# Statistics of two norms in a window-attention and Fourier kernel: one matmul with constant weights, an extra column of queries and keys, and row sums placed ahead of the keys

## The chip, the cores and the metric

The kernel runs on one core of a Trainium2 chip. Its time is device microseconds from the first to the last instruction of an execution; the median of several executions is compared. The engines of the core have names that come back in every profile line: PE (TensorE, matrix products; PEld is its loading of weights), DVE (VectorE), ACT (ScalarE), POOL (GpSimd) and SP (which here only issues DMAs). Each engine works through its own instructions in order and waits for others through semaphores.

## The reference, cut to what matters

The input x has 32 images of 56 x 56 positions with 128 channels, in 32-bit floats. Two layers are applied, each as x = x + layer(group norm of x):

```
def _gn(v, G=32, eps=1e-5):        # 32 groups of 4 channels
    m, s = mean and variance over height, width and the 4 channels of a group
    return (v - m) / sqrt(s + eps)

x = x + window_attention(_gn(x))   # 7x7 windows, shifted by 3, 4 heads of 32
x = x + fourier_layer(_gn(x))      # 32 cosine modes along w and along h, then a feed-forward 128-512-128
```

In the attention q, k and v are linear in the normed input, without a bias of their own: q = Wq (x - m) r = (Wq r) x - (Wq r) m, where r is the reciprocal deviation of a channel's group. So the norm can be put into the weights (scaled by r) and a shift (the product of weights and -m r). The statistics of the second norm are sums and sums of squares over an image's result of the first layer.

## The kernel before, in words

An image is held as 28 chunks of 112 positions x 128 channels (`xl`, positions on partitions). `image_group` (L252) transposes one row of eight windows at a time into `xw` (channels on partitions, 392 positions, and 15 columns of zeros behind them) and takes statistics of each (`bn_stats`, L270).

The main loop (L857) runs in cycles, one for each row of windows: eight cycles per image, 256 in all, and a tail. A cycle overlaps several stages of a software pipeline. Row r gets queries, keys, values and scores in cycle r, is normalised by its softmax in cycle r+1, and is transposed, multiplied with the values, projected and added to `xl` in cycle r+2. In cycle r+3 its sums for the second norm are taken (`attn_sums`, instructions at L501 and L503). Beside that the Fourier layer of the image before (from cycle 10 on: `CONV_BEGIN`) and the feed-forward of the image before that are spread over the same cycles. The feed-forward (`ff_in`, L688; `ff_out`, L708) takes part in cycles with numbers 7 to 10 and 12 to 14 of an image's Fourier schedule, which runs over 16 cycles, so in the steady state in seven cycles of eight.

The order on PE, ACT, DVE and POOL is written out by hand: the instructions run in the order in which the functions emit them (L850). `full_first` (L764) opens a cycle: transposes of the attention weights (`attn_transpose`, L411 to L421), queries and keys (`attn_qk`), a step of the first norm of the next image, the row sums (`attn_sums`), the statistics of the second norm where the image's Fourier layer begins (`fourier_stats`), the first half of the feed-forward, and the softmax's division (`attn_divide`, L397 to L400). Then come the scores (L367) with their eviction on DVE (L375), the values (L345), the Fourier transforms and mixes, and last the second half of the feed-forward and the projection (L478) with its eviction into `xl` (L486).

PSUM is used through two rings of four banks each: `pa` for the attention and both norms, `pc` for the Fourier layer and the feed-forward.

The places that the change touches:

- `image_norm` (L278): a chain of small steps, spread over two cycles before an image's first row. Group means by a matmul with `gavg` (L284), deviations, group variance by another (L295), `rstd` by POOL (L299), `nb` = -mean x rstd (L301), weights `wn` = `wqkv` x rstd on ACT (L306), then three matmuls of one column each for the shifts of q, k and v (L309), and DVE writes the five columns of `bqkv` from them (L313 to L315): shift of q times its scale, of k, of v, and of k masked for even and odd heads.
- `attn_qk` (L319): a 392-column matmul for q (L323) and for k (L328). ACT evicts q (L324) and half of k (L330) with their shifts as bias; DVE evicts the other half of k (L333).
- `attn_sums`: ACT squares the piece (L501), then DVE reduces the piece and the squares, both by line L503, into `part`.
- `fourier_stats`: DVE adds the eight rows (`tot`, L513) and copies each group's sums to its four channels (`totc`, L521). Two matmuls with `totc` as weights and a single column `gmean` give mean and mean square per channel (L525). DVE copies them (`ms`, L533) and goes on to the variance (L535, L539), POOL gives `rstd` (L543), DVE the shift (L545).

Of the kernel before, what the change touches and what calls it, by code (L numbers as in the profile page):

```python
# [10 lines left out]
F32 = mybir.dt.float32  # L11
AF = mybir.ActivationFunctionType
ALU = mybir.AluOpType
AX = mybir.AxisListType

P = 128
S = 56
C = 128
# [12 lines left out]
TC = 2 * S  # L31
# [17 lines left out]
def swin_fourier_kernel(  # L49
# [166 lines left out]

    gmean = const.tile([TC, 1], F32, tag="gmean", name="gmean")
    nc.gpsimd.memset(gmean, 1.0 / (4 * NT))
# [59 lines left out]
    def image_norm(im):  # L278
# [6 lines left out]
        gm = small.tile([P, 1], F32, tag="gm", name="gm")  # L285
        nc.vector.tensor_copy(gm, pg[:, 0:1])
        d = small.tile([P, 1], F32, tag="d", name="d")
        nc.vector.tensor_tensor(d, mv[:, 0:1], gm, ALU.subtract)
# [18 lines left out]
        pb = attn_bank()  # L307
        for j in range(3):
            nc.tensor.matmul(  # L309
                pb[:, j : j + 1], lhsT=wqkv[:, j * C : (j + 1) * C], rhs=nb, start=True, stop=True  # L310
            )
        im.bias = small.tile([P, 5], F32, tag="bqkv", name="bqkv")
        nc.vector.tensor_scalar(im.bias[:, 0:1], pb[:, 0:1], QS, None, ALU.mult)  # L313
        nc.vector.tensor_copy(im.bias[:, 1:3], pb[:, 1:3])
        nc.vector.tensor_scalar(im.bias[:, 3:5], heads, im.bias[:, 1:2], None, ALU.mult)  # L315
        yield


    def attn_qk(im, i):  # L319

        q, src = q_sb, im.xw[i][:, :RT]
        pq = attn_bank()
        nc.tensor.matmul(pq[:, :RT], lhsT=im.w[:, 0:C], rhs=src, start=True, stop=True)  # L323
        nc.scalar.activation(  # L324
            q[:, :RT], pq[:, :RT], AF.Identity, bias=im.bias[:, 0:1], scale=QS
        )
        pk = attn_bank()
        nc.tensor.matmul(pk[:, :RT], lhsT=im.w[:, C : 2 * C], rhs=src, start=True, stop=True)  # L328
        pk3 = pk[:, :RT].rearrange("p (w j) -> p w j", j=WT)
# [166 lines left out]
    def attn_sums(im, i):  # L496

        n0, n1 = WS * i // 2, WS * (i + 1) // 2
        piece = im.x[:, n0:n1]
        sq = work.tile([TC, 4, C], F32, tag="sq", name="sq", bufs=1)  # L500
        nc.scalar.activation(sq[:, : n1 - n0], piece, AF.Square)  # L501
        for k, src in ((0, piece), (1, sq[:, : n1 - n0])):
            nc.vector.tensor_reduce(  # L503
                im.part[:, k, :, i],
                src.rearrange("p n (g c) -> p g n c", c=4),
                axis=AX.XY,
                op=ALU.add,
            )


    def fourier_stats(im):
# [6 lines left out]
        )  # L518

        totc = small.tile([TC, 2, C // 4, 4], F32, tag="totc", name="totc", bufs=1)  # L520
        nc.vector.tensor_copy(totc, tot.unsqueeze(3).to_broadcast([TC, 2, C // 4, 4]))  # L521
        yield
        pg = attn_bank()
        for k in range(2):
            nc.tensor.matmul(  # L525
                pg[:, k : k + 1],
                lhsT=totc[:, k].rearrange("p g c -> p (g c)"),
                rhs=gmean,
                start=True,
                stop=True,  # L530
            )
        ms = small.tile([P, 2], F32, tag="ms", name="ms")
        nc.vector.tensor_copy(ms, pg[:, 0:2])  # L533
        nm2 = small.tile([P, 1], F32, tag="nm2", name="nm2")
# [215 lines left out]
    def row(r):  # L750
        return (images[r // NWR], r % NWR) if 0 <= r < NB * NWR else (None, 0)
# [12 lines left out]
    def full_first(cycle, norm):  # L764
        im, i = row(cycle - 2)
        if im:
            attn_transpose(im, i, cycle - 2)
        im, i = row(cycle)
        if im:
# [4 lines left out]
        next(norm)  # L774
        im, i = row(cycle - 3)
        if im:
            attn_sums(im, i)
        for im, c in fourier(cycle):
# [160 lines left out]
```

## Time and profile before

| what | value |
|---|---|
| time, median of 3 runs | 3755.23 us (3753.02 to 3755.56) |
| span of the profiled execution | 3748.9 us |
| mean granted PE clock | 0.993 |
| q and k matmuls (L323, L328) | 512 passes each, mean 509 and 506 ns |
| bias matmuls (L309) | 192 passes, mean 244 ns |
| statistics matmuls of the second norm (L525) | 128 passes, mean 251 ns; PE idle before them 17.2 us |
| row sums (L503), 384 and 512 wide | 545 ns and 678 ns, 128 each of piece and squares |
| keys on DVE (L333) | 256 of 685 ns; DVE idle before them 420.0 us |

A matmul of 32-bit floats shows as two passes, each with a weight load (PEld) that overlaps the passes around it. In a line of the profile `out<-in` gives the tiles by the program's names, then shapes, then how many instructions stand behind the line; what follows the bar is busy time, the mean of one, and the engine's idle time just before it with what ended it. In a timeline the columns are start and length in us, engine, line, operation, and in brackets the idle time before. DMA queues are busy 36.7% of the span.

### The profile page before, as it was taken

What the parts mean: (1) busy time and instruction counts of PE and PEld (TensorE: products, weight loads), DVE (VectorE), ACT (ScalarE), POOL (GpSimd) and SP (SyncE); (2) the same over time, 40 slices, a digit from 0 to 9 for tenths busy, and PEclk for the clock granted to TensorE, in tenths of its full rate; (3) what the DMA queues carried; (4) which work ended last, traced back from release to release, by engine and by line L of the source; (5) the groups of instructions that cost most, each with busy time, mean ns of one, the idle gap of its engine ahead of it and who ended that gap; (6) DMA issues with size and microseconds to landing.
All of it is one profiled execution on the core that took longest, in us unless ns stands there. A gap on an engine that the chain in (4) does not pass through costs nothing.

```text
span 3748.9 us, 140497 instructions
## 1 busy us (share of the span) xinstructions
PE 3658.2 (98%) x61632; PEld 2985.1 (80%) x61632; DVE 2197.3 (59%) x4619; ACT 2131.1 (57%) x3809; POOL 1370.9 (37%) x1421
## 2 busy tenths in 40 slices
PE   6799999999999999999999999999999999999998
PEld 5678888888888788888878888888887888888776
DVE  6665665556655556655556655666556566655641
ACT  3455556555565556555555565555655555655553
POOL 4333343333434333343334333333343333333321
PEclk8899999999999999999999999999999999999999
DMA  4233334334333434343343343343333333433332
GB/s 111 78 100 106 107 91 116 105 103 114 91 111 105 110 99 112 96 110 106 104 111 100 98 115 104 100 114 94 110 105 107 103 112 92 115 106 104 94 104 89
DMA packets 687779, 388.95 MB, mean 104 GB/s; under 512 B 40479, under 2 KB 658112, under 8 KB 686912
## 3 DMA queue, kind: packets, MB, share of 16 engines
q1 hardware_dynamic: 686557, 379.65, 36.7%
q8 instruction: 485, 7.95, 0.9%
q14 instruction: 126, 1.03, 0.1%
q10 hardware_dynamic: 611, 0.32, 0.0%
HBM read 218.29 MB, written 161.48 MB: 101 GB/s over the span
## 4 chain that ended last, share of the span: by engine, by line
PE 88%; DVE 7%; ACT 2%; DMA 1%; issue 1%; POOL 0%; SPq 0%; ACTq 0%; POOLq 0%; DVEq 0%
PE pc L708 20%; PE pc L688 15%; PE pa L345 7%; PE pc L572 6%; PE pc L606 5%; PE pa L367 5%; PE pa L411 5%; PE pa L478 5%; PE pc L645 5%; PE pa L436 4%; PE pa L323 4%; PE pa L328 4%; PE pa L259 2%; DVE part L503 1%; DVE st L270 1%; DVE a L375 1%
## 5 line engine op out<-in xcount | busy, mean ns | idle before, releaser
L400 POOL TENSOR_TENSOR a<-a,rs 128x784 f32<-128x784 f32 x256 | 389.5, 1521 | 1366.7 <-DVE rs L399 1254.4
L708 PE MATMUL pc<-wff,hid 128*128 128x128 f32 (+1 forms) x6400 | 778.2, 279 | 0.9 <-ACT hid L696 0.7
L708 PEld LDWEIGHTS pc<-wff,hid 128*128 128x128 f32 (+1 forms) x6400 | 731.0, 189 | 21.0 <-issue 1.9
L688 PE MATMUL pc<-xf,wff 128*128 128x512 f32 (+2 forms) x1792 | 712.8, 540 | 0.0
L696 ACT ACTIVATE hid<-pc,b1sb 128x512 f32<-128x512 f32 (+2 forms) x896 | 540.9, 634 | 102.0 <-PE pc L688 98.7
L688 PEld LDWEIGHTS pc<-xf,wff 128*128 128x128 f32 x1792 | 337.1, 190 | 300.4 <-issue 229.5
L386 POOL TENSOR_TENSOR a<-a,mx 128x784 f32<-128x784 f32 x256 | 389.0, 1520 | 389.2 <-DVE mx L385 384.7
L717 DVE TENSOR_TENSOR res<-pc,res 128x512 f32<-128x512 f32 (+2 forms) x256 | 143.5, 571 | 597.1 <-issue 269.8
L333 DVE TENSOR_SCALAR k<-pa,heads,bqkv 128x392 f32<-128x392 f32 x256 | 175.4, 685 | 420.0 <-ACT k L330 419.9
L419 ACT COPY aT<-pa 113x452 f32<-113x452 f32 x256 | 137.3, 536 | 475.4 <-PE pa L411 475.3
L274 POOL TENSOR_TENSOR xl<-xl,bproj 112x384 f32<-112x384 f32 (+1 forms) x256 | 291.4, 1139 | 227.3 <-PE pa L259 224.2
L392 ACT ACTIVATE a<-a 128x784 f32<-128x784 f32 x256 | 222.6, 869 | 203.5 <-POOL a L386 202.3
L375 DVE TENSOR_TENSOR a<-pa,bm 128x392 f32<-128x392 f32 x512 | 259.5, 549 | 132.1 <-PE pa L367 132.1
L352 ACT COPY v<-pa 128x512 f32<-128x512 f32 x256 | 152.4, 595 | 295.6 <-PE pa L345 295.6
L467 DVE TENSOR_SCALAR oT<-pa,bqkv 128x98 f32<-128x98 f32 (+2 forms) x768 | 171.1, 279 | 248.0 <-PE pa L436 248.0
L678 POOL TENSOR_TENSOR res<-res,b2sb 128x512 f32<-128x512 f32 (+2 forms) x256 | 263.8, 1036 | 101.0 <-DMA res<-scr 101.0
L367 PEld LDWEIGHTS pa<-k,q 64*64 64x64 f32 x8192 | 184.0, 133 | 142.7 <-issue 52.9
L345 PE MATMUL pa<-wn,xw 128*64 128x128 f32 x4096 | 282.1, 280 | 1.1 <-ACT aT L419 1.1
L345 PEld LDWEIGHTS pa<-wn,xw 128*64 128x64 f32 x4096 | 220.0, 137 | 55.3 <-issue 21.9
L478 PE MATMUL pa<-wproj,oT 128*112 128x128 f32 x1792 | 239.3, 274 | 14.3 <-DVE oT L467 11.3
L411 PE MATMUL pa<-ident,a 113*113 113x113 f32 x2048 | 250.0, 265 | 1.5 <-POOL a L400 1.5
L367 PE MATMUL pa<-k,q 64*64 64x98 f32 x8192 | 233.4, 250 | 18.5 <-DVE k L333 18.5
(87 smaller groups left out, 5939.7 us busy)
## 6 DMA issues: line engine op xcount, KB each, us to landing
zscr<-z SPq DMA_DIRECT2D x512, 112.0 KB
htok<-scr SPq DMA_DIRECT2D x256, 196.0 KB
zT<-zscr SPq DMA_DIRECT2D x192, 256.0 KB
res<-scr SPq DMA_DIRECT2D x160, 256.0 KB
out_dram<-res SPq DMA_DIRECT2D x128, 256.0 KB
scr<-xl SPq DMA_DIRECT2D x128, 224.0 KB
xl<-in_x_dram SPq DMA_DIRECT2D x32, 784.0 KB
xl<-in_x_dram SPq DMA_DIRECT2D x32, 672.0 KB
```

What stands on the lines that cost most here:

```text
L274: nc.gpsimd.tensor_tensor(piece, piece, bproj.unsqueeze(1).to_broadcast([TC, n1 - n0, C]), ALU.add)
L345: nc.tensor.matmul(pv[hs, j * C : (j + 1) * C], lhsT=im.xw[i][:, w * WT : w * WT + JP], rhs=im.w[:, 2 * C : 3 * C], start=True, stop=True,)
L367: nc.tensor.matmul(ps[hp][HALVES[e], pr * 2 * WT : (pr + 1) * 2 * WT], lhsT=q[cs, w * WT : w * WT + JP], rhs=k_sb[cs, :, w], start=True, s ...
L375: nc.vector.tensor_tensor(a[:, 2 * hp : 2 * hp + 2, :, 0:WT].rearrange("p u w j -> p w u j"), ps[hp][:, :RT].rearrange("p (w u j) -> p w u ...
L386: nc.gpsimd.tensor_tensor(a3, a3, mx.unsqueeze(2).to_broadcast([P, 2 * NWR, WT]), ALU.subtract)
L400: nc.gpsimd.tensor_tensor(a3, a3, rs.unsqueeze(2).to_broadcast([P, 2 * NWR, WT]), ALU.mult)
L411: nc.tensor.transpose(pt[:PW, h * P : h * P + PW], a[:PW, h, 2 * hf : 2 * hf + 2].rearrange("p w j -> p (w j)")[:, :PW], ident[:PW, :PW],)
L478: nc.tensor.matmul(pp[:TC, (n - n0) * C : (n - n0 + 1) * C], lhsT=oT[:, (n - base) * TC : (n - base + 1) * TC], rhs=wproj, start=True, sto ...
L678: nc.gpsimd.tensor_tensor(res[:m, c0:c1], res[:m, c0:c1], b2sb[:m].unsqueeze(1).to_broadcast([m, c1 - c0, C]), ALU.add,)
L688: nc.tensor.matmul(ph[:, :n], lhsT=wff1[:, f * P : (f + 1) * P], rhs=xff[:, t0 : t0 + n], start=True, stop=True,)
L696: nc.scalar.activation(hf[:, :n], ph[:, :n], AF.Relu, bias=b1sb[:, f : f + 1])
L708: nc.tensor.matmul(pf[:m, c * C : (c + 1) * C], lhsT=im.hid[f][:, c * P : c * P + m], rhs=wff2[:, f], start=(f == 0), stop=(f == NF - 1),)
```

## The change

There are three edits.

1. The second norm's statistics. `gmean` becomes a 112 x 128 block of one constant and is the weights; `tot` itself (64 columns: 32 sums, 32 sums of squares) is streamed, by one matmul in place of two. Every channel then holds all 64 group values; DVE multiplies them by a mask of the channel's own group (from `gavg`, with its 0.25 undone by a factor 4) and reduces to the two values. The copy `totc` goes.
2. The first norm's shifts of q and k. Minus the group mean is written as column 392 of the first row's `xw`, so that the q and k matmuls of that row, made 393 columns wide, give the shifts as their last column. ACT takes these from PSUM into `bqkv`: one small operation ahead of q, two ahead of k, in the first row of each image alone. Only the shift of v keeps its own matmul.
3. The row sums. `attn_sums` becomes a generator in two parts. The reduce of the piece itself is emitted between `attn_transpose` and `attn_qk`, so that on DVE it stands between `aT` and the keys; the squares on ACT and their reduce stay where they were.

The order of the instructions on PE, POOL and SP is the same but for the matmuls that are left out.

```diff
@@ -214,7 +214,7 @@
     mhalf = const.tile([P, 1], F32, tag="mhalf", name="mhalf")
     nc.gpsimd.memset(mhalf, -0.5)
 
-    gmean = const.tile([TC, 1], F32, tag="gmean", name="gmean")
+    gmean = const.tile([TC, P], F32, tag="gmean", name="gmean")
     nc.gpsimd.memset(gmean, 1.0 / (4 * NT))
 
 
@@ -284,6 +284,8 @@
         nc.tensor.matmul(pg[:, 0:1], lhsT=gavg, rhs=mv[:, 0:1], start=True, stop=True)
         gm = small.tile([P, 1], F32, tag="gm", name="gm")
         nc.vector.tensor_copy(gm, pg[:, 0:1])
+
+        nc.vector.tensor_scalar(im.xw[0][:, RT : RT + 1], gm, -1.0, None, ALU.mult)
         d = small.tile([P, 1], F32, tag="d", name="d")
         nc.vector.tensor_tensor(d, mv[:, 0:1], gm, ALU.subtract)
         e = small.tile([P, 1], F32, tag="e", name="e")
@@ -305,27 +307,28 @@
         yield
         nc.scalar.mul(im.w, wqkv, rstd)
         pb = attn_bank()
-        for j in range(3):
-            nc.tensor.matmul(
-                pb[:, j : j + 1], lhsT=wqkv[:, j * C : (j + 1) * C], rhs=nb, start=True, stop=True
-            )
+        nc.tensor.matmul(pb[:, 0:1], lhsT=wqkv[:, 2 * C :], rhs=nb, start=True, stop=True)
         im.bias = small.tile([P, 5], F32, tag="bqkv", name="bqkv")
-        nc.vector.tensor_scalar(im.bias[:, 0:1], pb[:, 0:1], QS, None, ALU.mult)
-        nc.vector.tensor_copy(im.bias[:, 1:3], pb[:, 1:3])
-        nc.vector.tensor_scalar(im.bias[:, 3:5], heads, im.bias[:, 1:2], None, ALU.mult)
+        nc.vector.tensor_copy(im.bias[:, 2:3], pb[:, 0:1])
         yield
 
 
     def attn_qk(im, i):
 
-        q, src = q_sb, im.xw[i][:, :RT]
+        n = RT if i else RT + 1
+        q, src = q_sb, im.xw[i][:, :n]
         pq = attn_bank()
-        nc.tensor.matmul(pq[:, :RT], lhsT=im.w[:, 0:C], rhs=src, start=True, stop=True)
+        nc.tensor.matmul(pq[:, :n], lhsT=im.w[:, 0:C], rhs=src, start=True, stop=True)
+        if i == 0:
+            nc.scalar.mul(im.bias[:, 0:1], pq[:, RT:n], QS)
         nc.scalar.activation(
             q[:, :RT], pq[:, :RT], AF.Identity, bias=im.bias[:, 0:1], scale=QS
         )
         pk = attn_bank()
-        nc.tensor.matmul(pk[:, :RT], lhsT=im.w[:, C : 2 * C], rhs=src, start=True, stop=True)
+        nc.tensor.matmul(pk[:, :n], lhsT=im.w[:, C : 2 * C], rhs=src, start=True, stop=True)
+        if i == 0:
+            for u in range(2):
+                nc.scalar.mul(im.bias[:, 3 + u : 4 + u], pk[:, RT:n], heads[:, u : u + 1])
         pk3 = pk[:, :RT].rearrange("p (w j) -> p w j", j=WT)
         nc.scalar.activation(
             k_sb[:, 0], pk3, AF.Identity, bias=im.bias[:, 3:4], scale=heads[:, 0:1]
@@ -497,15 +500,22 @@
 
         n0, n1 = WS * i // 2, WS * (i + 1) // 2
         piece = im.x[:, n0:n1]
-        sq = work.tile([TC, 4, C], F32, tag="sq", name="sq", bufs=1)
-        nc.scalar.activation(sq[:, : n1 - n0], piece, AF.Square)
-        for k, src in ((0, piece), (1, sq[:, : n1 - n0])):
-            nc.vector.tensor_reduce(
-                im.part[:, k, :, i],
-                src.rearrange("p n (g c) -> p g n c", c=4),
-                axis=AX.XY,
-                op=ALU.add,
-            )
+        nc.vector.tensor_reduce(
+            im.part[:, 0, :, i],
+            piece.rearrange("p n (g c) -> p g n c", c=4),
+            axis=AX.XY,
+            op=ALU.add,
+        )
+        yield
+        sq = work.tile([TC, 4, C], F32, tag="sq", name="sq", bufs=1)[:, : n1 - n0]
+        nc.scalar.activation(sq, piece, AF.Square)
+        nc.vector.tensor_reduce(
+            im.part[:, 1, :, i],
+            sq.rearrange("p n (g c) -> p g n c", c=4),
+            axis=AX.XY,
+            op=ALU.add,
+        )
+        yield
 
 
     def fourier_stats(im):
@@ -516,21 +526,29 @@
             axis=AX.X,
             op=ALU.add,
         )
-
-        totc = small.tile([TC, 2, C // 4, 4], F32, tag="totc", name="totc", bufs=1)
-        nc.vector.tensor_copy(totc, tot.unsqueeze(3).to_broadcast([TC, 2, C // 4, 4]))
         yield
         pg = attn_bank()
-        for k in range(2):
-            nc.tensor.matmul(
-                pg[:, k : k + 1],
-                lhsT=totc[:, k].rearrange("p g c -> p (g c)"),
-                rhs=gmean,
-                start=True,
-                stop=True,
-            )
+
+        nc.tensor.matmul(
+            pg[:, : C // 2],
+            lhsT=gmean,
+            rhs=tot.rearrange("p k g -> p (k g)"),
+            start=True,
+            stop=True,
+        )
+        own = small.tile([P, 2, C // 4], F32, tag="own", name="own", bufs=1)
+        nc.vector.scalar_tensor_tensor(
+            out=own,
+            in0=pg[:, : C // 2].rearrange("p (k g) -> p k g", k=2),
+            scalar=4.0,
+            in1=gavg.rearrange("p (g c) -> p g c", c=4)[:, :, 0]
+            .unsqueeze(1)
+            .to_broadcast([P, 2, C // 4]),
+            op0=ALU.mult,
+            op1=ALU.mult,
+        )
         ms = small.tile([P, 2], F32, tag="ms", name="ms")
-        nc.vector.tensor_copy(ms, pg[:, 0:2])
+        nc.vector.tensor_reduce(ms, own, axis=AX.X, op=ALU.add)
         nm2 = small.tile([P, 1], F32, tag="nm2", name="nm2")
         nc.vector.scalar_tensor_tensor(
             out=nm2, in0=ms[:, 0:1], scalar=-1.0, in1=ms[:, 0:1], op0=ALU.mult, op1=ALU.mult
@@ -765,6 +783,10 @@
         im, i = row(cycle - 2)
         if im:
             attn_transpose(im, i, cycle - 2)
+        last, j = row(cycle - 3)
+        if last:
+            sums = attn_sums(last, j)
+            next(sums)
         im, i = row(cycle)
         if im:
             attn_qk(im, i)
@@ -772,9 +794,8 @@
             for width, g in back_groups(c):
                 load_modes(im, width, g)
         next(norm)
-        im, i = row(cycle - 3)
-        if im:
-            attn_sums(im, i)
+        if last:
+            next(sums)
         for im, c in fourier(cycle):
             if c == 0:
                 im.stats = fourier_stats(im)
```

## The prediction, on record before the changed kernel ran

> **What bounds the kernel now.** I read the page from its busy shares down, then the chain of work that ended last, then PE's waits, then the timeline around the places that the change touches.
>
> ```profile
> PE 3658.2 (98%) x61632; PEld 2985.1 (80%) x61632; DVE 2197.3 (59%) x4619; ACT 2131.1 (57%) x3809; POOL 1370.9 (37%) x1421
> ...
> PE   6799999999999999999999999999999999999998
> PEclk8899999999999999999999999999999999999999
> ```
>
> TensorE is busy 98% and every slice after the second is full. So an edit is worth what it takes off PE, plus the PE waits it shortens. Time saved on DVE or ACT alone is worth nothing. The chain that ended last says the same: PE 88%, DVE 7%, ACT 2%. The first two slices (187 us) are the exception: there PE waits for others and is granted 0.8 of its clock. PE's waits:
>
> ```profile
> PE pa L367 <- DVE k L333: 18.5, 15, 2.9
> PE pa L525 <- DVE totc L521: 17.2, 31, 3.9
> PE pa L478 <- DVE oT L467: 11.3, 7, 2.5
> ```
>
> The second line is the statistics of the second norm, once per image; the others belong to the start. The columns are total us, times, longest. Now the timeline of one cycle that holds these statistics (start, us, engine, line, idle before):
>
> ```profile
> 1134.02 3.60 PE L688 MATMUL pc<-xf,wff 128*128 128x512 f32 x8
> 1134.29 0.68 ACT L330 ACTIVATE k<-pa,bqkv,heads 128x392 f32<-128x392 f32 x1
> 1134.86 0.62 ACT L501 ACTIVATE sq<-xl 112x512 f32<-112x512 f32 x1
> 1135.00 0.69 DVE L333 TENSOR_SCALAR k<-pa,heads,bqkv 128x392 f32<-128x392 f32 x1 [1.67 <-ACT k L330]
> 1135.60 0.68 DVE L503 TENSOR_REDUCE part<-xl 112x32 f32<-112x512 f32 x1
> 1136.19 0.68 DVE L503 TENSOR_REDUCE part<-sq 112x32 f32<-112x512 f32 x1
> 1136.91 0.69 DVE L513 TENSOR_REDUCE tot<-part 112x64 f32<-112x512 f32 x1
> 1137.63 0.29 DVE L521 COPY totc<-tot 112x256 f32<-112x256 f32 x1
> 1138.07 0.58 PE L525 MATMUL pa<-gmean,totc 112*128 112x1 f32 x4 [0.45 <-DVE totc L521]
> 1138.57 0.71 PEld L367 LDWEIGHTS pa<-k,q 64*64 64x64 f32 x32
> ```
>
> DVE stands idle 1.67 us before the keys. Then four DVE instructions run nose to tail, and PE waits for the last. From the start of L688 to the start of the scores (L367) is 4.55 us here. In the cycle before, which has no statistics, the same pair starts at 1120.08 and 1123.61: 3.53 us. So the statistics cost PE 1.02 us per image. Both spacings repeat within 5 ns in the other images. Last, the turn into an image's first row:
>
> ```profile
> 1216.04 1.04 PE L478 MATMUL pa<-wproj,oT 128*112 128x128 f32 x8
> 1216.91 0.73 PE L309 MATMUL pa<-nb,wqkv 128*128 128x1 f32 x6
> 1217.50 1.03 PE L411 MATMUL pa<-ident,a 113*113 113x113 f32 x8
> 1219.94 0.68 ACT L330 ACTIVATE k<-pa,bqkv,heads 128x392 f32<-128x392 f32 x1
> 1220.66 0.69 DVE L333 TENSOR_SCALAR k<-pa,heads,bqkv 128x392 f32<-128x392 f32 x1 [1.86 <-ACT k L330]
> 1223.22 0.71 PEld L367 LDWEIGHTS pa<-k,q 64*64 64x64 f32 x32 [0.76 <-issue]
> ```
>
> The bias matmuls hold PE 0.59 us (1216.91 to 1217.50), and the keys are ready at 1221.35, 1.87 us before the scores ask for them.
>
> **What the Trainium skill says.** "TensorE: Matmul & The Clock Gate", LDWEIGHTS, prices a weight load at columns/1.2 ns, about 107 ns for 128 columns whatever is streamed. The trace agrees: six one-column passes in 0.59 us are 98 ns each. So one-column matmuls cost a weight load per pass. The same page (Part 1) says an idle PE falls to half clock for windows of about 3.4 us. L323 to L328 takes 0.67 us in steady state and 1.33 us at 102.03 (1.33 = 103.36 - 102.03), so the start does run partly at half speed. "PSUM — Partial Sum Buffer" reports that ScalarE and VectorE reads of one bank collide; it fits that DVE's keys always begin after ACT's have ended (255 of 256 waits there are on ACT k). "ScalarE: Activation LUTs", What ACT_TABLE_LOAD costs: 186 ns + 0.833 per element, 93 ns more for each pointer operand. The oT eviction of 196 elements with a pointer bias gives 442 ns by that; the trace has 447.
>
> **The change part by part**, against the profiled span of 3748.9 us. The three timed runs have a median of 3755.23; I take the difference off that.
>
> (1) Statistics, PE's waits. Removed ahead of the matmul on DVE: totc's copy (0.29), and the xl reduce (0.55 or 0.68) moves up into the idle time before the keys. That idle time is never under 1.1 us from the fourth image on (1.67 in this cycle), since the keys wait for ACT; aT, in front of the reduce, is done by 1133.33. So the keys are not delayed. Sums of squares can start at 1135.69 (keys done; sq is done at 1135.48), tot ends at 1137.1, and PE comes free at 1134.02 + 3.44 = 1137.46 (3.44 is L688's spacing where its successor doesn't wait). The wait goes to zero with 0.2 to 0.3 us to spare.
>
> (2) Statistics, PE's work. Four passes of one column become two passes of 64 columns. The nearest rows: L284's two passes put 0.14 us between L328 and L688 (0.80 against 0.66). Four passes of L525 hold PE 0.51, two fewer at 98 ns leave 0.31, and 64 columns may not hide fully behind the next load: at 0.84 ns per column (L688: 0.43 us per 512) two passes add at most 0.11. I take 0.33, bounds 0.31 and 0.42. So L688 to scores becomes 3.44 + 0.33 = 3.77 instead of 4.55: 0.78 us. Thirty images wait like this: 23.4 us; the last doesn't wait, 0.2.
>
> Behind the matmul DVE gains `own` (64 elements, about 0.23) and a reduce of 64 (0.2, from 0.54 at 384 and 0.68 at 512) in place of a copy of 0.16: +0.27, then rstd on POOL. rstd was ready at 1139.86 and the first y eviction began at 1141.43. With PE 0.78 earlier the margin is still near 1 us. Free.
>
> (3) Bias by extra columns. L309 loses four of six passes: 4 x 98 = 0.39 us, 31 times 12.2 us; the first image's, at half clock, about 0.5 more. A 393rd column is 2 x 2 passes x 0.84 ns = 3 ns per image: nothing. On DVE three small operations become one and the -gm write (about 0.15) is added; its waits, for gm and for POOL's memset two cycles earlier, are over by then, and behind it only d and e move, which PE needs half a cycle later (L295). On ACT three operations are added in row 0: 0.19 + 0.28 + 0.28 = 0.75 us by the skill's price, bounds 0.5 and 0.9, ahead of q and k. Queued behind them are sq and the four hid evictions, whose banks the mode matmuls (L645) want. Keys have 1.87 us of slack, covered by L688's 3.6 us; the hid evictions have 0.17 us of idle each and catch up. So free for 29 or 30 images. Images 1 and 2 have no feed-forward between keys and scores and lose about 0.6 each: -1.2.
>
> (4) Row sums first, elsewhere. In steady cycles free and worthless, as PE doesn't wait for DVE there. At the start it does: L478 waits for oT (11.3), L259 and L295 for the score eviction (4.7), and DVE runs gapless from the keys to oT. Each such cycle shortens by the reduce, 0.55 to 0.68; rows 0 to 6 of the first image and cycle 16 are eight: 4.9. Its statistics at 128.75 waited 3.88 and gain 0.68 + 0.29, plus 0.2 of passes: 1.1. Bounds for this part: 0, and 14 if fewer stretches run at half clock (20 us between 97 and 135 do).
>
> Order on PE, POOL and SP does not change, and no DMA moves. Sum: 23.6 + 12.7 - 1.2 + 6.0 = 41.1 us, so 3755.2 - 41.1 = **3714**.
>
> **Rivals.**
> (a) The statistics' wait is replaced: PE now waits as long for the sums of squares or tot. For: the margin is 0.2 to 0.3 us. Against: everything ahead of tot has its time in the timeline above. Without the 18 us (30 x 0.60): 3732.
> (b) The start gains more: shorter waits keep the clock up. Up to 8 us more: 3706. For: 20 us at half clock. Against: I can't tell where the 3.4 us windows fall.
> (c) Slower: the three ACT operations delay the keys past their slack in row 0. PE stalls 30 times by what exceeds 1.87 us. The gain of 41 us is gone at 1.37 us of stall, that is 3.2 us for three operations, 1.08 each; a table load (1.28 us, once in the trace) in each would do it: 0.75 + 3.85 - 1.87 = 2.7 us, 30 times, 3796. Against: scaled copies already run between Exp and Identity with one table load in all.
> (d) It does not do what it says: another wait takes over just behind (conv banks, rstd), and little is left: about 3750.
>
> **How the numbers follow.** Main forecast 0.72 (its own range 3708 to 3722); (a) 0.08; (b) 0.13; (c) 0.03; (d) 0.04. 0.2% (7.5 us) is about what a measurement of this kernel tells from no change. Of (d), a quarter is faster, half the same, a quarter slower: faster 0.94, same 0.02, slower 0.04. Range 3701 to 3730: it takes in (b) and part of (a).
>
> **What the profile after would show.** L525's successor without PE idle before it, and L688 to scores at about 3.77 us; the bias matmul's block 0.2 us instead of 0.59; DVE idle before keys down from 420 us to about 270; three ACT rows of 0.2 to 0.3 us in row 0 with no new PE wait for k there; the period per image, now 113.7 to 114.6 us from first row to first row, shorter by 1.17 us. I'd be wrong if the two 64-column passes cost much more than 0.33, if the wait for tot stays, or if row 0 shows a PE wait for DVE k.

## The result and the profile after

The changed kernel takes 3713.97 us (median of 4 runs, 3712.71 to 3715.27), the kernel before 3755.39 us beside it: ratio 0.9891, 95% interval [0.9874, 0.9908]. The forecast was 3714. The profiled execution has a span of 3710.8 us against 3748.9.

First the page of the changed kernel, busy shares, slices and one group; the group's columns are count, busy us, mean ns, idle us before it and what ended that.

```profile
PE 3631.9 (98%) x61440; PEld 2967.1 (80%) x61440; DVE 2187.3 (59%) x4587; ACT 2140.9 (58%) x3905; POOL 1370.9 (37%) x1421
...
PE   6799999999999999999999999999999999999998
...
L336 DVE TENSOR_SCALAR k<-pa,heads,bqkv 128x392 f32<-128x392 f32 x256 | 175.2, 685 | 295.6 <-ACT k L333 295.6
```

PE is as full as before, with 26 us less busy time; the rest is less idle time. DVE's idle time ahead of the keys fell from 420.0 to 295.6 us (about 270 forecast): the row sums went into it, and the keys still wait for ACT, as they did. PE's waits in the changed kernel:

```profile
PE pa L370 <- DVE k L336: 18.7, 13, 4.0
PE pa L481 <- DVE oT L470: 9.6, 8, 1.7
...
PE pa L532 <- DVE tot L523: 3.7, 1, 3.7
```

L532 is the new statistics matmul. It waits once, in the first image, where the old one waited 31 times. The waits for keys and oT belong to the start, as before. Now the timeline of one cycle with the statistics, the same stage as shown of the kernel before:

```profile
1116.65 0.68 DVE L503 TENSOR_REDUCE part<-xl 112x32 f32<-112x512 f32 x1
1117.43 3.60 PE L706 MATMUL pc<-xf,wff 128*128 128x512 f32 x8
1118.40 0.69 DVE L336 TENSOR_SCALAR k<-pa,heads,bqkv 128x392 f32<-128x392 f32 x1 [1.08 <-ACT k L333]
1119.00 0.68 DVE L512 TENSOR_REDUCE part<-sq 112x32 f32<-112x512 f32 x1
1119.72 0.69 DVE L523 TENSOR_REDUCE tot<-part 112x64 f32<-112x512 f32 x1
1120.86 0.33 PE L532 MATMUL pa<-tot,gmean 112*128 112x64 f32 x2
1121.12 0.71 PEld L370 LDWEIGHTS pa<-k,q 64*64 64x64 f32 x32
```

`tot` is ready at 1120.41, and PE comes to its matmul 0.45 us later, without a wait. From L706 to the scores it is 3.69 us (4.55 before, 3.77 forecast). And the turn into an image's first row:

```profile
1199.46 0.28 PE L310 MATMUL pa<-nb,wqkv 128*128 128x1 f32 x2
1199.60 1.02 PE L414 MATMUL pa<-ident,a 113*113 113x113 f32 x8
1199.66 0.69 DVE L489 TENSOR_TENSOR xl<-pa,xl 112x512 f32<-112x512 f32 x1
1200.47 0.30 PEld L321 LDWEIGHTS pa<-xw,wn 128*128 128x128 f32 x2
1200.50 0.90 PE L321 MATMUL pa<-xw,wn 128*128 128x393 f32 x2
1201.23 0.82 PE L328 MATMUL pa<-xw,wn 128*128 128x393 f32 x2
1201.43 0.17 ACT L323 ACTIVATE bqkv<-pa 128x1 f32<-128x1 f32 x1 [0.17 <-PE pa L321]
1202.12 0.41 ACT L331 ACTIVATE bqkv<-pa,heads 128x1 f32<-128x1 f32 x2
1203.13 0.69 DVE L336 TENSOR_SCALAR k<-pa,heads,bqkv 128x392 f32<-128x392 f32 x1 [1.58 <-ACT k L333]
1205.42 0.71 PEld L370 LDWEIGHTS pa<-k,q 64*64 64x64 f32 x32 [0.76 <-DVE sm L400]
```

The bias matmul holds PE 0.14 us (0.59 before). The keys are ready at 1203.82, 1.60 us before the scores begin; the 0.76 us in front of PEld is there in undelayed cycles too, while the last wide pass of the feed-forward runs.

One thing is new here. The projection's eviction into `xl` (L489) ends at 1200.35, and the first weight load of the queries (L321) begins 0.12 us later. In the kernel before 0.46 us lay between the two:

```profile
1217.11 0.69 DVE L486 TENSOR_TENSOR xl<-pa,xl 112x512 f32<-112x512 f32 x1
1218.27 0.30 PEld L323 LDWEIGHTS pa<-xw,wn 128*128 128x128 f32 x2
```

The distance is 0.115 or 0.116 us in thirty images. The ring of four `pa` banks gives the reason: projection, bias and the two transposed halves take one bank each, so the queries get the projection's bank again and must wait until it has been read. No run moved the eviction by itself; the reading rests on the fixed distance and on this order of the banks. The wait is new, and it gives back part of what the bias matmuls gained.

Where the time came from can be read off the starts of the queries' matmul, row by row, in the two timelines. From row 24 to row 248, 28 steady images, it is 3190.95 us before and 3159.02 after: 31.9 us, 1.14 per image (1.17 forecast). From row 0 to row 24 it is 286.3 and 279.0: 7.3 us, the start and two images' worth of the same. Ahead of row 0 and behind row 248 the changed kernel loses 1.2 us, which leaves the 38.1 us between the two spans; the medians of the timed runs differ by 41.4.

By the median of each row over the steady images, three rows of eight changed: row 2, with the statistics, from 16.87 to 16.01 us; row 7, with the bias matmul at its end, from 13.30 to 12.89; and row 0 from 14.11 to 14.18, by the new wait. That makes 1.20 us per image. Pauses of PE, which a later section takes up, account for the difference to 1.14.

### The profile page after: what moved, and what is told of

The parts are those of the page before. It is cut to its first block, busy times and chain, and to the rows that moved or that the text cites. A ratio compares the mean times of both kernels' runs of the same rounds, so it can differ in the third digit from the quotient of the medians.

```text
span 3710.8 us, 139943 instructions
## 1 busy us (share of the span) xinstructions
PE 3631.9 (98%) x61440; PEld 2967.1 (80%) x61440; DVE 2187.3 (59%) x4587; ACT 2140.9 (58%) x3905; POOL 1370.9 (37%) x1421
## 4 chain that ended last, share of the span: by engine, by line
PE 92%; DVE 4%; DMA 1%; ACT 1%; issue 0%; POOL 0%; SPq 0%; ACTq 0%; POOLq 0%; DVEq 0%
PE pc L726 20%; PE pc L706 18%; PE pa L348 7%; PE pc L590 6%; PE pc L624 6%; PE pa L370 5%; PE pa L414 5%; PE pc L663 5%; PE pa L481 5%; PE pa L328 5%; PE pa L439 4%; PE pa L321 4%; PE pa L259 2%; DVE a L378 1%; DVE st L270 1%; DMA zscr<-z 1%
## 5 line engine op out<-in xcount | busy, mean ns | idle before, releaser
L706 PE MATMUL pc<-xf,wff 128*128 128x512 f32 (+2 forms) x1792 | 713.1, 540 | 0.8 <-ACT z L632 0.8
L706 PEld LDWEIGHTS pc<-xf,wff 128*128 128x128 f32 x1792 | 337.1, 190 | 301.4 <-issue 229.4
L336 DVE TENSOR_SCALAR k<-pa,heads,bqkv 128x392 f32<-128x392 f32 x256 | 175.2, 685 | 295.6 <-ACT k L333 295.6
L696 POOL TENSOR_TENSOR res<-res,b2sb 128x512 f32<-128x512 f32 (+2 forms) x256 | 263.1, 1033 | 103.4 <-DMA res<-scr 93.0
L481 PE MATMUL pa<-wproj,oT 128*112 128x128 f32 x1792 | 239.3, 274 | 11.3 <-DVE oT L470 9.6
```

What stands on the lines that cost most here:

```text
L481: nc.tensor.matmul(pp[:TC, (n - n0) * C : (n - n0 + 1) * C], lhsT=oT[:, (n - base) * TC : (n - base + 1) * TC], rhs=wproj, start=True, sto ...
L696: nc.gpsimd.tensor_tensor(res[:m, c0:c1], res[:m, c0:c1], b2sb[:m].unsqueeze(1).to_broadcast([m, c1 - c0, C]), ALU.add,)
L706: nc.tensor.matmul(ph[:, :n], lhsT=wff1[:, f * P : (f + 1) * P], rhs=xff[:, t0 : t0 + n], start=True, stop=True,)
```

## Each edit by itself

**Edit 1 alone** (constant weights; row sums left behind the keys):

```diff
-    gmean = const.tile([TC, 1], F32, ...)
+    gmean = const.tile([TC, P], F32, ...)
...
-        nc.vector.tensor_copy(totc, tot.unsqueeze(3)...)
-        for k in range(2): matmul(pg[:, k : k + 1], lhsT=totc[:, k], rhs=gmean)
+        matmul(pg[:, : C // 2], lhsT=gmean, rhs=tot)     # and own, ms as in the change
```

> The kernel before with edit 1 alone: one statistics matmul with constant weights, row sums where they were. Theory (PE is the bound; an edit is worth PE time plus PE waits it shortens): only the copy totc (0.29 us and its gap) leaves the DVE run ahead of the matmul, so PE's wait goes from 0.60 to about 0.28 us; the two passes after it hold PE 0.26 us instead of 0.51. Together 0.57 us per image, 30 times 17, and 1 at the start: 3737 us. Rival (the matmul's own passes are all there is to gain, the wait stays): 8 us, 3747. Rival (the whole wait was totc): 26 us, 3729.

Measured: 3735.5 us, ratio 0.9954 [0.994, 0.9967], 15.9 us under the kernel before (3751.44 beside it). Its timeline in a cycle with the statistics:

```profile
1130.39 3.60 PE L696 MATMUL pc<-xf,wff 128*128 128x512 f32 x8
1131.36 0.68 DVE L333 TENSOR_SCALAR k<-pa,heads,bqkv 128x392 f32<-128x392 f32 x1 [1.67 <-ACT k L330]
1131.96 0.68 DVE L503 TENSOR_REDUCE part<-xl 112x32 f32<-112x512 f32 x1
1132.56 0.68 DVE L503 TENSOR_REDUCE part<-sq 112x32 f32<-112x512 f32 x1
1133.27 0.69 DVE L513 TENSOR_REDUCE tot<-part 112x64 f32<-112x512 f32 x1
1134.10 0.41 PE L522 MATMUL pa<-tot,gmean 112*128 112x64 f32 x2
1134.43 0.91 PE L367 MATMUL pa<-k,q 64*64 64x98 f32 x32
```

L696 to L522 takes 3.71 us. In the changed kernel the same distance is 3.43, in the kernel before 4.04 (medians over the images). So 0.28 us of waiting is left, though the view of waits names no wait here: L696's end is modelled, at 1133.99, and the gap to the next start is 0.11. Only the distance between starts shows it. The rivals, all of the wait and none of it, both fall. The two passes hold PE 0.34 us here, not the 0.26 expected.

**Edit 2 alone** (extra column for the shifts of q and k; the two others as before):

> The kernel before with edit 2 alone: the shifts of q and k as an extra column, three small ACT operations in an image's first row. Theory: four of six weight loads leave PE, 0.39 us per image, 31 times 12, nothing given back in steady rows 0 because the keys' slack there is 1.9 us: 3743 us; the block from the bias matmul to the transposes takes 0.2 us instead of 0.59. Rival (the three ACT operations show up as a wait for the keys): no gain or a loss, 3755 or more, and PE idle before the scores of row 0.

```diff
-        for j in range(3): matmul(pb[:, j : j + 1], lhsT=wqkv[:, j * C : (j + 1) * C], rhs=nb)
+        matmul(pb[:, 0:1], lhsT=wqkv[:, 2 * C :], rhs=nb)
+        n = RT if i else RT + 1                    # q and k matmuls n columns wide
+        if i == 0: nc.scalar.mul(...)              # one ahead of q, two ahead of k
```

Measured: 3741.39 us, ratio 0.9973 [0.9963, 0.9982], 10 us under; the image period is 0.35 us shorter. The block of the bias matmul is 0.14 us in steady state, and the scores of row 0 begin as long after the queries' matmul as before, but for 0.06 us: the keys' matmul starts 0.735 us after the queries', where it was 0.674. The 393rd column is not the reason. Each of the two matmuls has two passes; the first pass of the queries takes 0.405 us instead of 0.344, while the other three, just as wide, take 0.330 instead of 0.329. That first pass, and the transposes ahead of it (0.895 us instead of 0.861), are held by the projection's eviction as in the changed kernel: the queries' weights are loaded 0.12 us after its end. So 0.45 us leave the bias block, and 0.10 come back as this wait.

**Edit 3 alone** (the reduce of the piece between aT and the keys; old statistics):

> The kernel before with edit 3 alone: the reduce of the piece between aT and the keys on DVE. Theory: the DVE run ahead of the statistics matmul starts 0.68 us earlier and PE's wait of 0.60 us goes to about zero, 30 times: 18; the first image's DVE-bound rows give about 5: 3732 us. So edits 1 and 3 share the wait: the gains of the three alone add to about 53 us, more than the 41 of all together. Rival (gains are separate and add up): the three sum to 41 us, this one then about 12, 3743. Rival (the keys come later behind the reduce): slower than before.

```diff
         if im:
             attn_transpose(im, i, cycle - 2)
+        last, j = row(cycle - 3)
+        if last:
+            sums = attn_sums(last, j)
+            next(sums)                             # the reduce of the piece
...
-            attn_sums(im, i)
+            next(sums)                             # squares and their reduce
```

Measured: 3735.23 us, ratio 0.9951 [0.9937, 0.9964]: 16 us under by the medians, 18 by the ratio, where 23 were expected. The wait is gone all the same, as the timeline shows:

```profile
1126.42 3.60 PE L695 MATMUL pc<-xf,wff 128*128 128x512 f32 x8
1127.40 0.68 DVE L333 TENSOR_SCALAR k<-pa,heads,bqkv 128x392 f32<-128x392 f32 x1 [1.08 <-ACT k L330]
1128.00 0.68 DVE L509 TENSOR_REDUCE part<-sq 112x32 f32<-112x512 f32 x1
1128.71 0.69 DVE L520 TENSOR_REDUCE tot<-part 112x64 f32<-112x512 f32 x1
1129.43 0.29 DVE L528 COPY totc<-tot 112x256 f32<-112x256 f32 x1
1129.87 0.58 PE L532 MATMUL pa<-gmean,totc 112*128 112x1 f32 x4
```

L695 to the statistics is 3.45 us, 0.02 above the changed kernel. So edit 3 takes away 0.59 us of waiting, edit 1 0.33, and both together 0.61: they share one wait. By their times the three seem to add up (15.9 + 10.1 + 16.2 = 42.2, against 41.4 together), as the rival has it, but edit 3's run lost time elsewhere, which a section of its own takes up below. The interval of edit 3's ratio just reaches the 23 us, so the times alone don't settle it; the distances do.

**Edit 3 in the first image alone:**

> The kernel before with edit 3 for the first image alone; all others have both reduces behind the keys. Theory: rows 0 to 7 of the first image are DVE-bound and each gets shorter by the reduce of 0.55 to 0.68 us: about 5 us by the end of cycle 10, 3750 us, and the steady period stays at 113.7 to 114.6 us. Rival (the start's gain in the changed kernel came from PE's clock or from the input's arrival): nothing, 3755. Rival (the steady part is what edit 3 gives everywhere): also 3755.

```diff
-            next(sums)
+            if last.b == 0: next(sums)             # ahead of the keys
...
+            if last.b: next(sums)                  # all other images: behind them
             next(sums)
```

Measured: 3745.15 us, ratio 0.9979 [0.9971, 0.9987], 6.3 us under. Rows 0 to 24 take 279.8 us instead of 286.3, and the 28 steady images 3190.1 instead of 3190.95. So the start's gain comes from moving the row sums in the first image. In its other 31 images the edit gives only the wait of the statistics.

How it comes is not as expected. The rows don't each get shorter by one reduce: row 3 takes 2.0 us less, row 4 1.5 more, row 5 1.5 less, and row 10, with the first image's statistics, 4.4 less (14.11 us instead of 18.52). Of these 4.4 us only 0.6 is a shorter wait for the statistics (3.28 us instead of 3.88). The rest is PE's own blocks getting shorter: the scores' takes 0.84 us instead of 1.52, the values' 0.92 instead of 1.76. The mean granted clock from 90 to 140 us is 0.80 in the kernel before and 0.90 here. So a good part of the start's gain comes through PE's clock. The rival that put the gain down to the clock alone, and so expected nothing from this edit, falls by its number, but the clock is part of the answer.

## How much room was there

**`tot` made late by one DVE instruction:**

> The changed kernel with the reduce of the squares issued twice in an image's last row, so that tot ends 0.68 us later. Theory (DVE's tot releases the statistics matmul, with about 0.3 us to spare): PE waits 0.4 us per image there, 30 times 12 us: slower than the changed kernel by 12, 29 under the kernel before. Rival (something else holds the matmul, and DVE has room to spare): no difference.

```diff
+        for _ in range(2 if i == NWR - 1 else 1):
         nc.vector.tensor_reduce(im.part[:, 1, :, i], sq..., op=ALU.add)
```

Measured: 3727.09 us; the changed kernel beside it, once more: 3709.44. Ratios to the kernel before 0.993 [0.9914, 0.9943] and 0.9881 [0.9866, 0.9897]. So 17.6 us slower (12 expected). The wait is back:

```profile
1124.86 3.60 PE L707 MATMUL pc<-xf,wff 128*128 128x512 f32 x8
1126.44 1.40 DVE L513 TENSOR_REDUCE part<-sq 112x32 f32<-112x512 f32 x2
1127.87 0.69 DVE L524 TENSOR_REDUCE tot<-part 112x64 f32<-112x512 f32 x1
1128.70 0.41 PE L533 MATMUL pa<-tot,gmean 112*128 112x64 f32 x2 [0.25 <-DVE tot L524]
1129.04 0.90 PE L370 MATMUL pa<-k,q 64*64 64x98 f32 x32
```

L707 to L533 is 3.84 us, 0.41 above the changed kernel, out of 0.72 that tot comes later: the room was 0.3 us, as forecast. (PE starts 0.14 us after tot's end here, so not all of the 0.45 us between the two in the changed kernel was room.) The matmul's own block grew too, from 0.26 to 0.34 us. Thirty times 0.48, the two together, is 14.5 of the 17.6 us; the start takes 2 more.

The changed kernel's second profile, expected as follows, repeats the first: steady rows 3157.5 us (3159.0), the same distances at the statistics. It is 44 us under the kernel before, where 41 were expected. Of its 11 short pauses 7 fall on the same matmuls as in the first profile.

> The changed kernel once more, beside the next three on one chip: 41 us under the kernel before, and the same steady period of 112.8 us. It shows too whether PE's short pauses inside a block of matmuls (8 us in all in its first profile) fall on the same instructions again: they do if the instruction stream sets them, they move if the run does.

**ACT loaded in the first row:**

> The changed kernel with the two masked copies of the keys' shift issued seven times each, that is twelve more small ACT operations ahead of the keys in each image's first row, 0.20 us each: 2.46 us. Theory: the keys are ready 1.6 us before the scores ask for them, so PE waits about 0.9 us there; the feed-forward's four evictions queue behind, and the last of them releases its bank about 0.8 us before the modes ask for it, so PE waits up to 0.7 us more after the scores. 30 times 1.6: 48 us slower than the changed kernel, 7 slower than before. Rival (the keys alone count): 0.9 x 30 = 27 slower than the changed kernel, 14 under before. Rival (ACT has room for all): no difference to the changed kernel.

```diff
-            for u in range(2):
+            for u in 7 * (0, 1):
                 nc.scalar.mul(im.bias[:, 3 + u : 4 + u], pk[:, RT:n], heads[:, u : u + 1])
```

Measured: 3739.5 us, ratio 0.9969 [0.9957, 0.9981]: 13.6 us under the kernel before, where the changed kernel was 44 under. Row 0 in its timeline:

```profile
1101.54 2.23 ACT L331 ACTIVATE bqkv<-pa,heads 128x1 f32<-128x1 f32 x14
1104.38 0.68 DVE L336 TENSOR_SCALAR k<-pa,heads,bqkv 128x392 f32<-128x392 f32 x1 [3.41 <-ACT k L333]
1105.12 0.90 PE L370 MATMUL pa<-k,q 64*64 64x98 f32 x32 [0.20 <-DVE k L336]
1105.84 1.23 PE L663 MATMUL pc<-idctw,zT 64*64 64x112 f32 x36
1107.22 0.98 PE L663 MATMUL pc<-idctw,zT 64*64 64x112 f32 x28 [0.16 <-ACT hid L714]
```

Fourteen take 2.23 us, so twelve cost 1.82 and not the 2.46 assumed. PE waits 0.27 us for the keys and 0.66 us for the banks of the last evictions (the block L663 grows from 1.64 to 2.30 us, of which the view of waits shows 0.16). The sum, 0.93 x 30 = 28 us, is most of the loss of about 31. So rival (c) of the prediction is a real mechanism, which begins when the slack is used up: the change used about 0.3 us of 1.9. And the banks of the evictions give more of the loss than the keys. The time alone would have misled here: it fits the rival that the keys alone count (14 under), because the theory had priced the twelve operations too high.

## Where edit 3's missing time went

In edit 3's first profile the distance L695 to scores is right in every image, yet some transforms take longer. The timeline of PE alone in edit 3's run, near 1700 us:

```profile
1697.89 1.09 PE L345 MATMUL pa<-wn,xw 128*64 128x128 f32 x16
1698.82 2.74 PE L579 MATMUL pc<-dct_w,xl 112*64 112x64 f32 x88
1703.05 0.92 PE L579 MATMUL pc<-dct_w,xl 112*64 112x64 f32 x24 [1.50 <-issue]
```

PE stops in mid-block for 1.5 us, with no wait that the profile shows. I counted all such pauses (two neighbouring narrow matmuls of one block more than 0.35 us apart, from 300 to 3600 us): 14.4 us in edit 3's run against 5.6 in the kernel before. "Runtime: NRT & Kernel Launch", Instruction fetch mechanics, of the Trainium skill says that engines refill their instructions in 16 KiB blocks of 256. The trace agrees in number: PE's 123264 matmuls and weight loads, with 1036 semaphore and drain instructions between them, are 485 such blocks, and the page of edit 3's run counts 485 packets on that queue (packets, MB, share of the DMA engines' span):

```profile
q8 instruction: 485, 7.95, 0.9%
```

The same section calls this fetching hidden, or mostly so; here it isn't always. Two runs on it, the first the same program once more, the second with this edit on top:

> The kernel with edit 3 alone, again. In its first profile PE paused 14.4 us in all inside blocks of matmuls with no wait to show, against 5.6 in the kernel before, and each pause came 1 to 4 us after a 16384-byte packet of the instruction queue; that is why its gain was 16 us where 23 were expected. Theory (PE's instruction blocks arrive late at fixed places of the stream): the pauses fall on the same matmuls again and sum to 10 us or more. Rival (a disturbed execution): other places, about 5 us, and a time nearer 3730.

> The kernel with edit 3 alone and the first image's 32 transposes issued twice, so that everything behind them on PE stands 128 instructions later in the stream; at most 4 us of PE work are added at the start, beside the input's loading. Theory (pauses belong to blocks of 256 instructions, which are 16384 bytes): the pauses leave the places they had, above all the long ones in the transforms (0.9 to 1.7 us), and come elsewhere, with another sum. Rival (the pauses belong to moments with much DMA traffic): the same places of the program, the same sum of 14 us.

```diff
-        for c in range(4):
+        for c in range(4) if im.b else 2 * (0, 1, 2, 3):
             nc.tensor.transpose(pt4...)
```

Repeated, edit 3 takes 3733.2 us (0.9951 [0.9937, 0.9966]) and pauses 11.5 us; nine of its 14 pauses are on the very same matmuls as in the first run. The shifted program takes 3740.73 us (0.9969 [0.996, 0.9977]): the start is 8.4 us later, more than the 4 that I had allowed, and none of its 15 pauses falls where edit 3 had paused. Their sum, 11.3 us, is hardly another. The shift was 64 instructions, not 128: a transpose here is one pass with one weight load (61664 of each on the page, against 61632).

The traces say more when PE's instructions (weight loads, matmuls and the semaphore and drain instructions between them) are counted from the first one. Then the pauses are of two kinds. In the fourteen profiles of this case there are 188, and 93 of them come at place 193 or 194 of a block of 256 (counted from 0), some in every profile, the shifted program's included. In each of these 93, PE goes on 2.2 to 3.0 us after the last 16384-byte packet of the instruction queue began. The other 95 all come where a block of transposes or of inverse transforms goes on to its next PSUM bank (the ninth matmul of L259, the 33rd or 37th of L652 or its counterpart). In edit 3's run the profile names what each of its seven waited for, six times ACT and once a DMA.

So the 14.4 us were not all without a visible wait: 7.9 us (9 pauses) are of the first kind and 6.5 of the second; in the kernel before 3.3 and 2.4, in the repeat 9.0 and 2.6, in the shifted run 8.7 and 2.7. The first kind belongs to the blocks of the instruction stream, as the fixed place shows. That PE stands there because the next block comes late follows from the place and the packet together; no run changed the fetching itself. Taken off both spans, both kinds of pauses leave edit 3 alone a gain of 3743.3 - 3719.3 = 24 us, close to the 23 expected. Pauses of the first kind come to 1 to 9 us in the fourteen profiles (changed kernel 4.1 and 3.6), so a result within some 5 us is partly a matter of where the blocks fall.

## A version beyond the change

**One group matmul in the first norm:**

> The changed kernel with one group matmul of two columns in the first norm (mean, and variance + mean squared), in place of two of one column, placed behind the feed-forward's first half. Theory (a weight load on PE is what such a matmul costs): the block of the second matmul, 0.24 us per image, goes: 31 times 7.5 us, 48 us under the kernel before. Rival (the norm's longer DVE step or the new place makes PE wait in that row): no gain, 41.

```diff
+        nc.vector.scalar_tensor_tensor(out=mv[:, 1:2], in0=mv[:, 0:1], scalar=mv[:, 0:1], in1=mv[:, 1:2], op0=ALU.mult, op1=ALU.add)
...
-        nc.tensor.matmul(pg[:, 0:1], lhsT=gavg, rhs=mv[:, 0:1], start=True, stop=True)
+        nc.tensor.matmul(pg[:, 0:2], lhsT=gavg, rhs=mv, start=True, stop=True)
...
-        nc.tensor.matmul(pv[:, 0:1], lhsT=gavg, rhs=e, start=True, stop=True)
...                                                # and the step moved behind ff_in
```

Measured: 3704.53 us, ratio 0.9872 [0.9859, 0.9886], 49 under the kernel before; the interval overlaps that of the changed kernel beside it, and row 7 shows the gain more surely, 12.73 us instead of 12.89. Of the 0.24 us of the second matmul's block and 0.11 from the new place, 0.2 came back behind the projection: the projection's block grew by 0.13 us and the shift's matmul by 0.07, since PE was now early for `nb`.

**That, and the next image's statistics behind the projection's eviction:**

> The kernel with one group matmul, and the statistics of the next image's windows emitted on DVE behind the projection's eviction into xl. Theory: in the rows where the next image is read, the keys' PSUM bank waits for that eviction, which stands behind three statistics of 0.5 us; PE loses about 0.3 us per image between the queries and the feed-forward there (row 6: 0.24 between queries and keys, 0.1 behind the keys). That goes: 9 us more, 57 under the kernel before. Rival (PE's weight loads were not held by it, only their order showed it so): same as with one group matmul alone, 48. Rival (aT behind the statistics comes later and delays queries): slower than that.

```diff
-        nc.vector.bn_stats(im.st[:, i], xw)        # in image_group
...
+                image_stats(images[b + 1], j)      # behind attn_project
```

Measured: 3730.03 us, ratio 0.9938 [0.9925, 0.995]: 25 us slower than with one group matmul. Row 6 gained 0.25 us of the 0.34 that it was to gain between queries and feed-forward, and gave 0.12 back in the inverse transforms. But the statistics now stand between the eviction and aT:

```profile
1201.40 1.49 DVE L278 BATCH_NORM_STATS2 st<-xw 128x6 f32<-128x392 f32 x3
1203.68 0.62 DVE L426 COPY aT<-pa 113x452 f32<-113x452 f32 x1
1204.22 0.54 DVE L505 TENSOR_REDUCE part<-xl 112x32 f32<-112x384 f32 x1
1204.68 0.67 DVE L338 TENSOR_SCALAR k<-pa,heads,bqkv 128x392 f32<-128x392 f32 x1
1205.40 0.91 PE L372 MATMUL pa<-k,q 64*64 64x98 f32 x32 [0.55 <-DVE k L338]
```

Before, the statistics ran while DVE waited for the projection; now DVE waits idle for it and then runs all of them ahead of the keys, with no idle time left, and the scores wait in row 7, which grows by 0.63 us. Rows 5 to 7 together lose 0.66 us per image, some 20 of the 25 us; the pauses, 10.8 us against 3.8, give the rest. The rival expected here, a later aT, holds in its direction; but it is the keys that come late, not the queries.

**One group matmul, and no `nb`:**

> The kernel with one group matmul in the first norm, and the shift of v from the scaled weights and the column -gm instead of from the unscaled weights and nb; the DVE operation nb (1.12 us, held while POOL adds) goes. In the kernel with one group matmul PE waited 0.13 us for it behind the projection and the block of the shift's matmul was 0.07 longer. Theory: both go, 31 x 0.2 = 6 us: 55 us under the kernel before. Rival (PE then waits for the scaled weights from ACT instead): no gain over 49.

```diff
-        nc.vector.scalar_tensor_tensor(out=nb, in0=gm, scalar=-1.0, in1=rstd, op0=ALU.mult, op1=ALU.mult)
...
-        nc.tensor.matmul(pb[:, 0:1], lhsT=wqkv[:, 2 * C :], rhs=nb, start=True, stop=True)
+        nc.tensor.matmul(pb[:, 0:1], lhsT=im.w[:, 2 * C :], rhs=im.xw[0][:, RT : RT + 1], start=True, stop=True)
```

Measured: 3701.02 us, ratio 0.9863 [0.9846, 0.9879], 52 us under the kernel before (55 expected) and the fastest here, by its median; its interval overlaps those of the version above and of the changed kernel's second measurement. Both growths went, the projection's block is 0.87 us again, and row 7 takes 12.53 us where it took 12.89 in the changed kernel.

## Why the prediction was right, point by point

- *PE is the bound, and only PE time and PE waits count.* Shown: all three edits alone gain what they take off PE's path (edit 3 with its pauses taken off), and edit 3 outside the first image gives nothing but the statistics' wait.
- *(1) The wait of 0.60 us goes, with 0.2 to 0.3 to spare.* Shown by the distance of 3.43 us instead of 4.04, and by the late `tot`: room 0.3 us.
- *(2) The new matmul holds PE 0.33 us, at least 0.31.* It held 0.26: under my lower bound. The bound took two one-column passes off the old block; the old block had begun with a wait, and edit 1 alone, where tot is still late, shows 0.34. Off a wait the first weight load is hidden behind L706: it begins 0.34 us ahead of its matmul in the changed kernel, 0.03 in edit 1 alone.
- *(3) Four weight loads at 98 ns are 0.39 us.* The net was 0.35: the block shrank by 0.45, and 0.10 went to a wait that stood in no term, that of the queries for the projection's bank. It shows as 0.03 in the transposes and 0.06 in the queries' first pass. The 393rd column itself is free, as forecast.
- *(3) Three ACT operations delay the keys by 0.75 us, within 1.87 of slack.* The delay was about 0.3 us: they take 0.17 and 2 x 0.2 us, and part of it falls while ACT would wait for the keys' matmul. The term was too large, without effect in steady images. Images 1 and 2 lost 0.3 to 0.4 us each ahead of their scores with edit 2 alone, not 0.6.
- *(4) The start gains 6 us.* The first image alone gave 6.3, but not by one reduce in each of eight rows and 1.1 at the statistics: row 10 alone gave 4.4, most of it by PE's clock, which the term allowed for in its upper bound alone. That the size fits is luck.
- *The sum:* per steady image the statistics gave 0.85 us instead of 0.78 and the shifts 0.35 instead of 0.39, so 1.20 instead of 1.17 by the rows' medians, and 1.14 with the pauses, which were in no term (2.5 us between these two profiles). That the total came within 0.3 us of the forecast (41.4 against 41.1) is luck too: the two profiled spans differ by 38.1, and the second measurement gave 44.2.
- *Rival (a)* needs tot 0.3 us later, *(c)* needs more than 2 us of further ACT work (1.82 us left the kernel 13.6 us faster than before); neither was near. *(b)* came true in its mechanism, though not on top of the 6 us: between 20 and 300 us the granted clock was 0.5 for 43.5 us in the kernel before, for 35.7 and 34.1 in the two profiles of the changed kernel, for 33 to 34 with edit 3 alone, and for 45.4 and 41.2 with edit 1 or 2 alone. How much of the start's gain this is can't be told exactly; the second profile of the same program had a start 2 us longer than the first.

## What to carry to other kernels

Where PE is full, price an edit by the distance between starts of PE's blocks, with and without the instruction in question, and not by the idle time that the view of waits shows: modelled ends hide part of a short wait (0.45 us shown of 0.60) or all of it (0.28). Move work on an in-order engine into the idle time ahead of an instruction that waits for another engine, and check that the next engine's deadline is still met; statistics placed behind such a wait made the kernel 25 us slower here. When PE's block gets shorter, look for the next thing that it then has to wait for, such as the bank of an earlier result. A matmul of one column costs its weight loads, so shifts and statistics are cheapest as columns of matmuls that run anyway.

## What the runs showed of the hardware that was not expected

PE pauses of 0.3 to 1.7 us in mid-block come at place 193 or 194 of a block of 256 instructions, 93 times in fourteen profiles. Many return at the same matmuls in a repeated run of one program, and none did when the stream was shifted. PE goes on 2.2 to 3.0 us after a packet of the instruction queue began. Small ACT operations of one column with a scale per channel overlap: each takes 0.26 us, and in a row of fourteen one starts every 0.15 us (2.23 us in all). A 393rd column added 1 ns to a pass of 392 columns (0.330 us instead of 0.329).
